# Two of four expert weight buffers held in a finished input tensor, early rows loaded from ScalarE's queue, and loads of sums ahead of stores

## The chip, the cores and the metric

The kernel runs on one core of a Trainium2 chip. A core has five engines that work from queues of their own and wait for one another through semaphores: TensorE (PE) multiplies matrices, VectorE (DVE), ScalarE (ACT) and GpSimd (POOL) work on elements, and SyncE (SP) mainly starts transfers. Sixteen DMA engines move data between the device memory (HBM) and the on-chip memory (SBUF), which has 128 partitions. A DMA can be started from SP, ACT or POOL. The metric is the device time of one execution in microseconds (us), the median of several.

## The reference

A network of two layers, each with a mixing part and a part with experts, on x of 8 sequences x 512 tokens x 256 features in float32. Each part's output is added to its input and normalized:

```python
x = layernorm(x + L0_attn(x))   # three recurrent layers: conv, gates, scan, projection, rmsnorm
x = layernorm(x + L0_ffn(x))    # 8 experts, each takes its best T/8 tokens; a token keeps one expert
x = layernorm(x + L1_attn(x))   # 16-head attention, a relative bias added after the softmax, norm
x = layernorm(x + L1_ffn(x))    # 16 experts, each token uses its best 4
# L0_ffn, for the expert e of a token:  gate * (gelu(x @ W1[e]) @ W2[e])
# L1_ffn, over the four experts:  sum of c[e] * (gelu(x @ w1[e] + b1[e]) @ w2[e] + b2[e])
```

In both expert parts W1 is 256 x 512 and W2 is 512 x 256. T is 4096 tokens.

## The kernel before, in words

The tokens lie in SBUF as 32 chunks of 128 rows (`x_ext`: the features, then gates and indices). In an expert part, every token's row is written ("put", L721, an indirect DMA from POOL) into the list of its expert in HBM (`m0rows` in layer 0, `m1rows` in the last layer). A list is then worked off in tiles of 128 rows: 39 tiles in layer 0, 143 in the last layer. Empty rows (`none`) are written behind the end of each list by `end_list` (L758).

`Lists.run` (L830) works off the tiles of both layers. For tile t it needs the rows (`load`, L872 to L874, five buffers named `xg`) and the weights of the tile's expert (`weights`, L865 to L870, four buffers `ws` of 1.03 MB each: both matrices, the bias and a one-hot row). Which expert and which rows these are stands in a table in SBUF; `value` reads an entry into a register of SP, and the DMA uses it as its address. The first four tiles load weights unconditionally (L868), later ones only when the expert changes (L870). `turn` transposes the rows on PE and copies them (`xq`, L888); `first` makes 16 matmuls (L899) and four gelus on ACT (L905 with bias, L907 without); `second` makes eight matmuls (L921) and hands the result to `done`. In layer 0 `done` scatters it to `res` (L1131), in the last layer it adds it into `acc` in HBM (L1736), both by indirect DMA from POOL.

Both layers form part of their tiles early. In layer 0 the first eight tiles come from lists that hold only the first half of the tokens: once those 16 chunks' puts have landed, a copy on ACT (`m0full`, L740) releases the row loads. While those tiles run, the other puts go on, and later the ends are written. In the last layer the first 64 tiles come from the first five sequences, whose lists are formed while attention (L1441) still works on the other three. Attention's loop hands out small pieces of this routing work, "parts", between its own steps; the piece that belongs to sequence b is made by a function near L1318, and the last part of sequence 4 makes the early table.

The order of instructions on an engine is fixed when the kernel is built: by hand for attention's PE, ACT and DVE work and for POOL in `run`, and by a scheduler elsewhere. An engine starts its instructions in that order, so an instruction that waits holds up what follows. Completions of the DMAs from SP and ACT are counted on eight semaphores taken in turn: a DMA is issued only when the eighth before it has landed.

After the last tile, `token_choice_layer` (L1745 to L1761) loads the sums from `acc` in eight groups of four chunks (two loads a group, L1751, pool of six buffers for each of the two), adds them and the input with biases (L1756, L1757), normalizes (L59 to L68) and stores the group with four DMAs (L1761). `xT` is the layer's input transposed: two slabs (dc = 0, 1) of 4096 tokens along the free axis. It is read for the attention's projections and the routing of each sequence.

Of the kernel before, what the change touches and what calls it, by code (L numbers as in the profile page):

```python
# [10 lines left out]
F32 = mybir.dt.float32  # L11
# [6 lines left out]
P = 128  # L18
B, S, D = 8, 512, 256
T = B * S  # L20
NC = T // P
# [658 lines left out]
class Lists:  # L680
# [6 lines left out]
    def __init__(self, tc, ctx, name, E, NT, a):  # L687
        nc = tc.nc
        self.tc, self.nc, self.name, self.E, self.NT = tc, nc, name, E, NT
        rp = self.rp = ctx.enter_context(tc.tile_pool(name=f"{name}r", bufs=1))  # L690
        self.dram = ctx.enter_context(
            tc.tile_pool(name=f"{name}d", bufs=1, space=bass.MemoryType.DRAM)
        )
        self.rows = self.dram.tile([E * LT + P, RW], F32, name=f"{name}rows")
        self.written = []


        self.tabs, self.early, self.loads, self.grown = [], 0, [], None
        self.tri = rp.tile([P, P], F32, name=f"{name}tri")
        nc.sync.dma_start(self.tri, a["c_tri"])  # L700

        self.iot = rp.tile([P, E], F32, name=f"{name}iot")
        nc.sync.dma_start(self.iot, a["c_iota"][:E].partition_broadcast(P))
        self.pno = rp.tile([P, 1], F32, name=f"{name}pno")
        nc.sync.dma_start(self.pno, a["c_part"])
        self.pnw = rp.tile([P, 1], F32, name=f"{name}pnw")
        nc.vector.tensor_scalar_add(self.pnw, self.pno, -1.0)
        self.off = rp.tile([P, E], F32, name=f"{name}off")
        nc.vector.tensor_scalar_mul(self.off, self.iot, float(LT))
        self.ones = rp.tile([P, P], F32, name=f"{name}ones")  # L710
        nc.vector.memset(self.ones, 1.0)
        none = self.none = rp.tile([P, RW], F32, name=f"{name}none")
        nc.gpsimd.memset(none, 0.0)  # L713
        nc.gpsimd.iota(
            none[:, D + E1 : D + E1 + 2].bitcast(I32), pattern=[[0, 2]], base=T, channel_multiplier=1
        )
        nc.sync.dma_start(self.rows[E * LT :, :], none)
# [99 lines left out]
    def early_tiles(self):  # L817
# [9 lines left out]

        return 0.6, part

    def run(self, ctx, ident, w_pack, bias, done, taken=None, besides=None):  # L830

        tc, nc, E, NT, nm = self.tc, self.nc, self.E, self.NT, self.name
        wp = ctx.enter_context(tc.tile_pool(name=f"{nm}w", bufs=1))
        hp = self.hp
        psX = ctx.enter_context(tc.tile_pool(name=f"{nm}psX", bufs=2, space=PSUM))
        psH = ctx.enter_context(tc.tile_pool(name=f"{nm}psH", bufs=4, space=PSUM))
        psO = ctx.enter_context(
            tc.tile_pool(name=f"{nm}psO", bufs=1 if bias else 2, space=PSUM)  # L840
        )
        ws = [wp.tile([P, WPK], F32, name=f"{nm}ws{i}") for i in range(NW)]
        xgs, hTs = {}, {}

        def table(t):
            return [(t0, tab) for t0, tab in self.tabs if t0 <= t][-1]

        def entry(t):

            t0, _ = table(t)  # L850
            end = min([NT] + [self.early] * (t < self.early))
            i, k = divmod(t - t0, NW)
            size, more = divmod(end - t0, NW)
            return k * size + min(k, more) + i

        def value(t, n, hi):
            _, tab = table(t)
            i = entry(t)
            return nc.values_load_multi_w_load_instructions(
                tab[i : i + 1, n : n + 1],  # L860
                engines=[mybir.EngineType.SP], min_val=0, max_val=hi,
                skip_runtime_bounds_check_because="clamped where the table is made",
            )[1][0]

        def weights(t):  # L865
            w = w_pack.rearrange("e p f -> (e p) f")[bass.ds(value(t, 1, E * P - P), P), :]
            if t - table(t)[0] < NW:
                nc.sync.dma_start(ws[t % NW], w)  # L868
            else:
                nc.sync.dma_start(ws[t % NW], w, cond=value(t, 2, 1))  # L870

        def load(t):  # L872
            xgs[t] = hp.tile([P, RW], F32, tag="xg", bufs=NW + 1, name=f"{nm}xg_{t}")
            ins = nc.sync.dma_start(xgs[t], self.rows[bass.ds(value(t, 0, E * LT), P), :]).ins  # L874
            if t < self.early:

                for w in self.written:
                    tc.declare_no_dep(ins, w, reason="other rows, or before grown")
                tc.add_manual_dep(ins, self.grown.name, SYNC, reason="full tiles")
                self.loads.append(ins)  # L880

        def turn(t):
            xg = xgs[t]
            ps = psX.tile([P, DC, P], F32, tag="x", name=f"{nm}xp_{t}")
            for dc in range(DC):
                nc.tensor.transpose(ps[:, dc, :], xg[:, dc * P : (dc + 1) * P], ident)  # L886
            xq = hp.tile([P, DC, P], F32, tag="xq", name=f"{nm}xq_{t}")
            nc.vector.tensor_copy(xq, ps)  # L888
            xgs[t] = (xg, xq)

        def first(t):
            xg, xq = xgs[t]
            w = ws[t % NW]
            hT = hp.tile([P, FC, P], F32, tag="hT", name=f"{nm}hT_{t}")
            for fc in range(FC):
                ps = psH.tile([P, P], F32, tag="h", name=f"{nm}h_{t}_{fc}")
                for dc in range(DC):
                    o = dc * F + fc * P
                    nc.tensor.matmul(  # L899
                        ps, w[:, o : o + P], xq[:, dc, :],  # L900
                        start=(dc == 0), stop=(dc == DC - 1),
                    )
                o = DC * F + FC * D + fc
                if bias:
                    ins = nc.scalar.activation(hT[:, fc, :], ps, AF.Gelu, bias=w[:, o : o + 1])  # L905
                else:
                    ins = nc.scalar.activation(hT[:, fc, :], ps, AF.Gelu)  # L907
            hTs[t] = hT
            if taken:
                taken(t, xg, w)  # L910
                xgs[t] = None, None
            return ins.ins

        def second(t):
            xg, _ = xgs.pop(t)
            hT = hTs.pop(t)
            w = ws[t % NW]
            ps = psO.tile([P, D], F32, tag="o", name=f"{nm}o_{t}")
            for fc in range(FC):
                o = DC * F + fc * D  # L920
                nc.tensor.matmul(  # L921
                    ps, hT[:, fc, :], w[:, o : o + D], start=(fc == 0), stop=(fc == FC - 1)
                )
            done(t, xg, ps)


        for t in range(0 if bias else NW):
            weights(t)
        for t in range(NW):
            load(t)  # L930
            if bias:
                weights(t)
        turn(0)
        for t in range(NT + 1):
            if t < NT:
                ins = first(t)
            if t + 1 < NT:
                turn(t + 1)
            if t > 0:
                second(t - 1)  # L940
                if t + NW - 1 < NT:
                    load(t + NW - 1)
                    weights(t + NW - 1)
            if besides and t < NT:
                besides(t, ins)
# [211 lines left out]
class TokenChoice:  # L1157


    def __init__(self, tc, ctx, x_ext, xT, ident, eps5, acc, a):  # L1160
# [19 lines left out]
        self.eps3, self.eps5 = (ATT_EPS, e3), (LN_EPS, eps5)  # L1180
        self.rb = rp.tile([P, E1], F32, name="rb1")
        nc.sync.dma_start(self.rb, a["router_b"].partition_broadcast(P))
        self.b2_in = a["b2"]
        self.gam = rp.tile([P, D], F32, name="gam")
        nc.sync.dma_start(self.gam, a["gamma"].partition_broadcast(P))
        self.bet = rp.tile([P, D], F32, name="bet")
# [5 lines left out]
    def parts(self, b):  # L1192
# [125 lines left out]
        if b == SE - 1:  # L1318
            n, count = self.count("n6")
            L.done = L.rp.tile([P, E1], F32, name="done")  # L1320
            last = [count] + L.table(n, 0, 0) + [L.early_tiles()]
        return (
            [(0.0, beta)] + normalize_parts(nc, gp, ao, ao, G1, self.eps3, f"ao_{b}", b < SE)
            + [(0.0, gamma), None]
# [383 lines left out]
def token_choice_layer(R, w_pack, eps5, out):  # L1708

    tc, nc, L = R.tc, R.nc, R.L  # L1710
    with ExitStack() as ctx:
# [30 lines left out]
            L.run(tiles, R.ident, w_pack, True, done, taken, R.besides)  # L1742

        assert not R.rest
        fp = ctx.enter_context(tc.tile_pool(name="m1f", bufs=6))  # L1745
        psF = ctx.enter_context(tc.tile_pool(name="m1psF", bufs=3, space=PSUM))
        for g in range(NC // 4):
            ys = []
            for i in range(2):
                yt = fp.tile([P, 4, D], F32, tag=f"f{i}", name=f"f{i}_{g}")  # L1750
                nc.sync.dma_start(yt, R.sums[i][:, g * 4 : (g + 1) * 4, :])  # L1751
                ys.append(yt)
            ps = psF.tile([P, 4, D], F32, tag="f", name=f"xb_{g}")
            R.plus_biases(g, ps)
            y = ys[0]
            nc.vector.tensor_add(y, y, ys[1])  # L1756
            nc.vector.tensor_add(y, y, ps)  # L1757
            layernorm(nc, L.sm, y, y, 4, eps5, f"m1_{g}")
            rows = out[g * S : (g + 1) * S, :].rearrange("(i q e) d -> e i q d", q=G1, e=4)
# [116 lines left out]
```

## Time and profile before

| what | us |
|---|---|
| median of 3 runs | 2020.09 (2019.97 to 2020.74) |
| the profiled execution's own time | 2018.68 |
| its span | 2016.9 |
| PE busy | 1742.5 |
| DVE busy | 1135.0 |
| ACT busy | 1002.7 |
| POOL busy | 514.4 |
| mean granted TensorE clock | 0.926 |

The span runs from the first to the last recorded instruction; the profiled execution's time is a little longer than its span. A row of the timeline gives start and length in us, engine, line, operation, output and inputs, the number of instructions in it (x9) and, in brackets, how long the engine was idle before it and what released it. SPq is SP's own queue that starts DMAs: such a row tells when transfers were issued, not when they landed. PEld is the loading of weights into TensorE. The page's slices divide the span in 40 parts of 50.4 us, with a digit for the busy tenths of each.

### The profile page before, as it was taken

The page shows a single profiled execution, that of the slowest core. Times are in us where ns is not written, and L with a number is a line of the kernel's source. Part 1 is how long each engine was busy: PE and PEld are TensorE (multiplying, and loading weights), DVE is VectorE, ACT ScalarE, POOL GpSimd, SP SyncE. Part 2 cuts the span into 40 slices and gives each one's busy share as a digit, 9 for nine tenths or more (in the row PEclk, how much of TensorE's full clock was granted, in tenths as well). Part 3 has the DMA queues.
Part 4 walks back from the last instruction along what each step waited for, and adds up shares of the span by engine and source line. Part 5 has one row for each costly group of instructions (what it writes and reads, how often), then busy time and mean ns, then how long its engine had stood idle before and what let it go on. Part 6 is the DMA issues. An engine that isn't in the chain of part 4 may idle for free. (4 is left out here: it accounts for less than half of the span.)

```text
span 2016.9 us, 31168 instructions
## 1 busy us (share of the span) xinstructions
PE 1742.5 (86%) x10396; PEld 1136.3 (56%) x10396; DVE 1135.0 (56%) x2841; ACT 1002.7 (50%) x2167; POOL 514.4 (26%) x438
## 2 busy tenths in 40 slices
PE   7999995532799698999989999987999999999993
PEld 3555553331799493222222222223899989999983
DVE  6999998853122622676868776884434222222225
ACT  4899976500223411466666766655434333433333
POOL 1000000005222311001131422332666634444430
PEclk8999997655899797999999999998999999999997
DMA  9000000004644300000010111113776676656566
GB/s 358 34 0 1 1 0 1 32 7 172 234 136 139 109 1 21 14 16 15 25 53 16 57 47 31 54 45 115 197 172 135 144 190 142 137 116 144 109 157 181
DMA packets 107103, 179.66 MB, mean 89 GB/s; under 512 B 17005, under 2 KB 86847, under 8 KB 100160
## 3 DMA queue, kind: packets, MB, share of 16 engines
q1 hardware_dynamic: 73760, 129.45, 20.7%
q0 software_dynamic: 30176, 45.59, 11.5%
q10 hardware_dynamic: 3008, 2.63, 0.4%
q8 instruction: 84, 1.38, 0.3%
q14 instruction: 75, 0.61, 0.1%
HBM read 244.79 MB, written 62.98 MB: 153 GB/s over the span
## 5 line engine op out<-in xcount | busy, mean ns | idle before, releaser
L1677 DVE TENSOR_REDUCE nmx<-s 128x1 f32<-128x512 f32 x512 | 329.7, 685 | 162.2 <-PE t L1599 104.5
L1684 ACT ACTIVATE pe<-t 128x512 f32<-128x512 f32 x512 | 277.8, 594 | 210.1 <-PE t L1599 199.0
L905 ACT ACTIVATE m1hT<-m1h,m1ws 128x128 f32<-128x128 f32 x572 | 208.5, 367 | 308.9 <-PE m1h L899 270.9
L1587 PE MATMUL s<-kT,qT 32*128 32x512 f32 x1024 | 304.3, 669 | 54.5 <-ACT pe L1684 26.0
L1599 PE MATMUL t<-qA,kT 32*128 32x512 f32 x1024 | 293.2, 649 | 2.5 <-ACT pe L1684 2.0
L899 PEld LDWEIGHTS m1h<-m1xq,m1ws 128*128 128x128 f32 x2288 | 278.6, 193 | 12.6 <-issue 5.4
L1736 POOL DMA_INDIRECT acc<-y,at x143 | 221.0, 1546 | 250.8 <-DVE at L1729 189.9
L899 PE MATMUL m1h<-m1xq,m1ws 128*128 128x128 f32 x2288 | 281.7, 276 | 3.7 <-issue 2.2
L921 PE MATMUL m1o<-m1ws,m1hT 128*128 128x256 f32 x1144 | 273.4, 380 | 3.4 <-DVE at L1729 1.6
L921 PEld LDWEIGHTS m1o<-m1ws,m1hT 128*128 128x128 f32 x1144 | 205.6, 190 | 26.8 <-issue 3.6
L1587 PEld LDWEIGHTS s<-kT,qT 32*128 32x128 f32 x1024 | 81.9, 190 | 221.8 <-ACT pe L1684 173.6
L888 DVE COPY m1xq<-m1xp 128x256 f32<-128x256 f32 x143 | 60.5, 423 | 193.3 <-PE m1xp L886 114.4
L1735 DVE TENSOR_SCALAR y<-m1o,gt 128x256 f32<-128x256 f32 x143 | 69.1, 483 | 163.7 <-PE m1o L921 156.2
L721 POOL DMA_INDIRECT m1rows<-x_ext,slot x128 | 126.9, 992 | 119.7 <-ACT pe L1684 78.4
L1623 PE MATMUL po<-pe,V 128*17 128x512 f32 x1024 | 136.4, 605 | 1.2 <-ACT pe L1684 1.2
L1653 POOL TENSOR_TENSOR AO<-AO,on 128x256 f32<-128x256 f32 x32 | 23.5, 735 | 352.9 <-DVE on L1648 352.8
L907 ACT ACTIVATE m0hT<-m0h 128x128 f32<-128x128 f32 x156 | 42.9, 277 | 123.6 <-PE m0h L899 97.7
L713 POOL MEMSET m0none<- 128x276 f32 x1 | 0.3, 327 | 394.8 <-ACT table L673 394.8
L299 PE MATMUL gate<-xc,wi 128*128 128x512 f32 x192 | 92.2, 611 | 2.5 <-ACT junk L382 2.5
L299 PE MATMUL gate<-xc,wr 128*128 128x512 f32 x192 | 87.2, 608 | 7.2 <-issue 7.2
L899 PE MATMUL m0h<-m0xq,m0ws 128*128 128x128 f32 x624 | 79.9, 282 | 14.4 <-issue 11.8
L899 PEld LDWEIGHTS m0h<-m0xq,m0ws 128*128 128x128 f32 x624 | 78.2, 198 | 18.5 <-issue 16.3
(342 smaller groups left out, 2662.2 us busy)
## 6 DMA issues: line engine op xcount, KB each, us to landing
m1ws<-in_w_pack SPq DMA_DIRECT2D x143, 1034.0 KB
m0ws<-in_w_pack SPq DMA_DIRECT2D x39, 1034.0 KB
m1xg<-m1rows SPq DMA_DIRECT2D x143, 138.0 KB
acc<-zero SPq DMA_DIRECT2D x2, 4096.0 KB
f<-acc SPq DMA_DIRECT2D x16, 512.0 KB
m0xg<-m0rows SPq DMA_DIRECT2D x39, 138.0 KB
xT<-in_xT SPq DMA_DIRECT2D x4, 1024.0 KB
x_ext<-in_x SPq DMA_DIRECT2D x4, 1024.0 KB
```

The lines of the kernel that those rows point to most:

```text
L299: nc.tensor.matmul(ps, w[("wr", "wi")[g]][:, l, dc, oc * P : (oc + 1) * P], xcs[u][:, dc, b, :], start=(dc == 0), stop=(dc == DC - 1),)
L721: ins = self.nc.gpsimd.indirect_dma_start(out=self.rows[:, :], out_offset=bass.IndirectOffsetOnAxis(ap=place, axis=0), in_=row, in_offset= ...
L899: nc.tensor.matmul(ps, w[:, o : o + P], xq[:, dc, :], start=(dc == 0), stop=(dc == DC - 1),)
L905: ins = nc.scalar.activation(hT[:, fc, :], ps, AF.Gelu, bias=w[:, o : o + 1])
L921: nc.tensor.matmul(ps, hT[:, fc, :], w[:, o : o + D], start=(fc == 0), stop=(fc == FC - 1))
L1587: mm = nc.tensor.matmul(ps, qTs[u % NR][r, qc * P : (qc + 1) * P], kTs[u % NR][r, :], start=True, stop=True,)
L1599: mm = nc.tensor.matmul(ps, kTs[v % NR][r, kc * P : (kc + 1) * P], qAs[v][r, :], start=True, stop=True,)
L1623: mm = nc.tensor.matmul(po[h4 * HP : h4 * HP + VW, :], V[:, b * NQ + kc, 4 * g + h4, :], pes.pop((u, kc, h4)), start=(kc == 0), stop=(kc = ...
L1677: ins = nc.vector.tensor_reduce(at, ps, AX.X, ALU.max, negate=True)
L1684: ins = nc.scalar.activation(pe, ps, AF.Exp)
L1735: nc.vector.tensor_scalar_mul(y, ps, gt)
L1736: nc.gpsimd.indirect_dma_start(out=R.acc[t % 2][:, :], out_offset=bass.IndirectOffsetOnAxis(ap=at, axis=0), in_=y, in_offset=None, compute ...
```

## The change

1. Two of the last layer's four weight buffers are no longer allocated: they are the first 2068 columns (tokens 0 to 2067) of the two slabs of `xT`. The new method `hold` issues their first loads from SP as the last part of sequence 4's routing, in attention. `run` then allocates only the other two, and `weights` leaves out tiles 0 and 1. For that, the functions that read the table become methods (`of`, `value`, `weights_of`).
2. In layer 0 (`bias` is False), the row loads of the eight early tiles are issued from ACT instead of SP; each reads its address into a register of ACT first.
3. At the end, the pool of the sums has eight buffers for each of the two, and all sixteen loads are issued in a loop of their own, ahead of the groups' additions and stores.

By the built order of instructions, five of the eight row loads stand on ACT between the copy that releases them and the load of the gelu table; the sixth stands ahead of tile 3's gelus and waits for the scatter of result 0, since there are five row buffers; the seventh and eighth stand ahead of tile 4's gelus. On SP the ends of the lists come right behind the first four weight loads. In the last layer SP has both held loads in attention and then row loads 0, 1, 2, weights 2, rows 3, weights 3; the loads of the second biases, which stood between the first row load and the first weights, come around tile 20. On ACT the load of the gelu table and the gelus of the first two tiles come ahead of a normalization of four chunks (L124), which stood ahead of them.

```diff
@@ -696,6 +696,7 @@
         self.tabs, self.early, self.loads, self.grown = [], 0, [], None
+        self.held = []
         self.tri = rp.tile([P, P], F32, name=f"{name}tri")
         nc.sync.dma_start(self.tri, a["c_tri"])
@@ -827,11 +828,39 @@
         return 0.6, part
+    def of(self, t):
+        return [(t0, tab) for t0, tab in self.tabs if t0 <= t][-1]
+    def value(self, t, n, hi, engine=mybir.EngineType.SP):
+        t0, tab = self.of(t)
+        end = min([self.NT] + [self.early] * (t < self.early))
+        i, k = divmod(t - t0, NW)
+        size, more = divmod(end - t0, NW)
+        i += k * size + min(k, more)
+        return self.nc.values_load_multi_w_load_instructions(
+            tab[i : i + 1, n : n + 1],
+            engines=[engine], min_val=0, max_val=hi,
+            skip_runtime_bounds_check_because="clamped where the table is made",
+        )[1][0]
+    def weights_of(self, t, w_pack):
+        at = self.value(t, 1, self.E * P - P)
+        return w_pack.rearrange("e p f -> (e p) f")[bass.ds(at, P), :]
+    def hold(self, w_pack, at):
+        for t, dst in enumerate(at):
+            self.nc.sync.dma_start(dst, self.weights_of(t, w_pack))
+        self.held = at
     def run(self, ctx, ident, w_pack, bias, done, taken=None, besides=None):
         tc, nc, E, NT, nm = self.tc, self.nc, self.E, self.NT, self.name
+        table, value, weights_of = self.of, self.value, self.weights_of
         wp = ctx.enter_context(tc.tile_pool(name=f"{nm}w", bufs=1))
         hp = self.hp
         psX = ctx.enter_context(tc.tile_pool(name=f"{nm}psX", bufs=2, space=PSUM))
@@ -839,31 +868,16 @@
         psO = ctx.enter_context(
             tc.tile_pool(name=f"{nm}psO", bufs=1 if bias else 2, space=PSUM)
         )
-        ws = [wp.tile([P, WPK], F32, name=f"{nm}ws{i}") for i in range(NW)]
+        ws = [None] * len(self.held) + [
+            wp.tile([P, WPK], F32, name=f"{nm}ws{i}") for i in range(len(self.held), NW)
+        ]
+        ws[: len(self.held)] = self.held
         xgs, hTs = {}, {}
-        def table(t):
-            return [(t0, tab) for t0, tab in self.tabs if t0 <= t][-1]
-
-        def entry(t):
-
-            t0, _ = table(t)
-            end = min([NT] + [self.early] * (t < self.early))
-            i, k = divmod(t - t0, NW)
-            size, more = divmod(end - t0, NW)
-            return k * size + min(k, more) + i
-
-        def value(t, n, hi):
-            _, tab = table(t)
-            i = entry(t)
-            return nc.values_load_multi_w_load_instructions(
-                tab[i : i + 1, n : n + 1],
-                engines=[mybir.EngineType.SP], min_val=0, max_val=hi,
-                skip_runtime_bounds_check_because="clamped where the table is made",
-            )[1][0]
-
         def weights(t):
-            w = w_pack.rearrange("e p f -> (e p) f")[bass.ds(value(t, 1, E * P - P), P), :]
+            if t < len(self.held):
+                return
+            w = weights_of(t, w_pack)
             if t - table(t)[0] < NW:
                 nc.sync.dma_start(ws[t % NW], w)
             else:
@@ -871,7 +885,10 @@
         def load(t):
             xgs[t] = hp.tile([P, RW], F32, tag="xg", bufs=NW + 1, name=f"{nm}xg_{t}")
-            ins = nc.sync.dma_start(xgs[t], self.rows[bass.ds(value(t, 0, E * LT), P), :]).ins
+            q = nc.sync if bias or t >= self.early else nc.scalar
+            at = value(t, 0, E * LT, q.engine)
+            ins = q.dma_start(xgs[t], self.rows[bass.ds(at, P), :]).ins
             if t < self.early:
                 for w in self.written:
@@ -1180,7 +1197,7 @@
         self.eps3, self.eps5 = (ATT_EPS, e3), (LN_EPS, eps5)
         self.rb = rp.tile([P, E1], F32, name="rb1")
         nc.sync.dma_start(self.rb, a["router_b"].partition_broadcast(P))
-        self.b2_in = a["b2"]
+        self.b2_in, self.w_pack = a["b2"], a["w_pack"]
         self.gam = rp.tile([P, D], F32, name="gam")
         nc.sync.dma_start(self.gam, a["gamma"].partition_broadcast(P))
         self.bet = rp.tile([P, D], F32, name="bet")
@@ -1318,7 +1335,12 @@
         if b == SE - 1:
             n, count = self.count("n6")
             L.done = L.rp.tile([P, E1], F32, name="done")
-            last = [count] + L.table(n, 0, 0) + [L.early_tiles()]
+            at = [self.xT[:, dc, :WPK] for dc in range(DC)]
+            last = [count] + L.table(n, 0, 0) + [
+                L.early_tiles(), (0.0, lambda: L.hold(self.w_pack, at))
+            ]
         return (
             [(0.0, beta)] + normalize_parts(nc, gp, ao, ao, G1, self.eps3, f"ao_{b}", b < SE)
             + [(0.0, gamma), None]
@@ -1742,18 +1764,19 @@
             L.run(tiles, R.ident, w_pack, True, done, taken, R.besides)
         assert not R.rest
-        fp = ctx.enter_context(tc.tile_pool(name="m1f", bufs=6))
+        fp = ctx.enter_context(tc.tile_pool(name="m1f", bufs=NC // 4))
         psF = ctx.enter_context(tc.tile_pool(name="m1psF", bufs=3, space=PSUM))
+        ys = {}
         for g in range(NC // 4):
-            ys = []
             for i in range(2):
-                yt = fp.tile([P, 4, D], F32, tag=f"f{i}", name=f"f{i}_{g}")
-                nc.sync.dma_start(yt, R.sums[i][:, g * 4 : (g + 1) * 4, :])
-                ys.append(yt)
+                ys[g, i] = fp.tile([P, 4, D], F32, tag=f"f{i}", name=f"f{i}_{g}")
+                nc.sync.dma_start(ys[g, i], R.sums[i][:, g * 4 : (g + 1) * 4, :])
+        for g in range(NC // 4):
             ps = psF.tile([P, 4, D], F32, tag="f", name=f"xb_{g}")
             R.plus_biases(g, ps)
-            y = ys[0]
-            nc.vector.tensor_add(y, y, ys[1])
+            y = ys[g, 0]
+            nc.vector.tensor_add(y, y, ys[g, 1])
             nc.vector.tensor_add(y, y, ps)
             layernorm(nc, L.sm, y, y, 4, eps5, f"m1_{g}")
             rows = out[g * S : (g + 1) * S, :].rearrange("(i q e) d -> e i q d", q=G1, e=4)
```

## The prediction

> **What bounds the kernel now.** I read the page first. TensorE is busy for 86% of the span, so time can be won only where it stands idle for another reason. In the slices it does so in three places that the change touches: in the tenth and eleventh (454 to 554 us, digits 2 and 7: layer 0's experts start), in the 28th (1361 to 1411 us, digit 7: from attention into the last layer's experts) and in the last (3).
>
> ```profile
> PE 1742.5 (86%) x10396; PEld 1136.3 (56%) x10396; DVE 1135.0 (56%) x2841; ACT 1002.7 (50%) x2167; POOL 514.4 (26%) x438
> PE   7999995532799698999989999987999999999993
> ```
>
> Then the timeline of each place. First the end of the program, where nothing overlaps, so that a microsecond won is a microsecond of the span:
>
> ```profile
> 1959.07 4.35 SPq L1751 DMA_DIRECT2D f<-acc  x9
> 1973.33 16.10 SPq L1761 DMA_DIRECT2D out<-f  x20
> 1977.61 1.19 DVE L1756 TENSOR_TENSOR f<-f,f 128x1024 f32<-128x1024 f32 x1
> 1984.83 2.07 ACT L68 ACTIVATE f<-f,mr_m,rs_m 128x256 f32<-128x256 f32 x4 [0.44 <-DVE mr_m L66]
> 1989.48 2.77 SPq L1751 DMA_DIRECT2D f<-acc  x5
> 1994.97 1.22 DVE L1756 TENSOR_TENSOR f<-f,f 128x1024 f32<-128x1024 f32 x1 [10.18 <-DMA f<-acc]
> 2004.03 9.81 SPq L1761 DMA_DIRECT2D out<-f  x12
> 2008.99 2.07 ACT L68 ACTIVATE f<-f,mr_m,rs_m 128x256 f32<-128x256 f32 x4 [0.44 <-DVE mr_m L66]
> ```
>
> Nine loads of sums go out at once, then SP sits in 20 stores, each of which waits for its group's normalization, and only at 1989.48 come the five loads left. VectorE idles 10.18 us for them. Second, the start of the last layer's experts, in the timeline and in windows of 5 us (columns: length, busy time of PE, its weight load, DVE, ACT, POOL, granted clock, DMA share, GB/s):
>
> ```profile
> 1387.59 0.36 SPq L874 DMA_DIRECT2D m1xg<-m1rows  x1
> 1390.80 1.27 SPq L1415 DMA_DIRECT2D b<-in_b  x3
> 1394.28 0.36 SPq L868 DMA_DIRECT2D m1ws<-in_w_pack  x1
> 1400.06 3.73 PE L899 MATMUL m1h<-m1xq,m1ws 128*128 128x128 f32 x16
> 1401.38 1.28 ACT L905 ACT_TABLE_LOAD   x1 [0.30 <-ACT x_ext L124]
> 1390.00:1395.00 5.00, 1.51 (x6) 1.14 (x6) 4.10 (x19) 0.26 (x1) 2.38 (x3) 0.50 0.04 10
> 1395.00:1400.00 5.00, 0.39 (x2) 0.42 (x3) 4.89 (x44) 1.00 (x3) 0.00 (x0) 0.50 0.91 319
> 1400.00:1405.00 5.00, 5.00 (x24) 4.91 (x24) 3.13 (x24) 4.41 (x10) 0.00 (x0) 0.50 1.00 400
> ```
>
> The first weights are asked for at 1394.28, behind the bias loads and a release by POOL, and land at about 1400, when the first matmul starts. Third, layer 0's start:
>
> ```profile
> 490.69 12.70 SPq L874 DMA_DIRECT2D m0xg<-m0rows  x4
> 507.62 9.48 SPq L758 DMA_DIRECT2D m0rows<-m0none  x8
> 501.34 0.28 ACT L907 ACTIVATE m0hT<-m0h 128x128 f32<-128x128 f32 x1 [5.04 <-issue]
> 511.17 0.28 ACT L907 ACTIVATE m0hT<-m0h 128x128 f32<-128x128 f32 x1 [9.55 <-remote]
> 507.68 0.97 POOL L721 DMA_INDIRECT m0rows<-x_ext,slot  x1 [0.30 <-issue]
> 516.47 1.95 PE L899 MATMUL m0h<-m0xq,m0ws 128*128 128x128 f32 x16
> ```
>
> Four row loads take SP 12.7 us, while a later one takes about 0.86 with its address. ACT's gelus creep too, though matmuls are done. Both recover when POOL's last put (507.68) has landed; the profile names no releaser.
>
> **What the Trainium skill says.** "DMA: Bandwidth & Descriptors", section "Issuing engines are not separate DMA queues": starting DMAs from several engines saves only the sequencer's time, since all share the 16 DMA engines. So row loads on ACT can win no more than SP's issue time; here that is 12.7 us in a disturbed stretch. "PSUM — Partial Sum Buffer", section "Engine vs sequencer instructions": ScalarE's queue is strict FIFO; a load that waits holds up the gelus behind it. "TensorE: Matmul & The Clock Gate", Part 1: half clock until about 3.4 us of sustained work; the trace agrees (0.50 until 1405, sixteen L899 matmuls in 3.73 us against 1.95 warm).
>
> **The change, part by part.** All sums are against the profiled execution: 2018.68 us, span 2016.9, 1.41 us under the median of 2020.09.
>
> *Tail.* Sixteen loads go ahead of every store and have buffers of their own. Loads: 16 x 0.524 MB = 8.4 MB; the window 1965 to 1970 moves 415 GB/s, so they take 20.2 us and the last lands, some 2 us of start added, at about 1981. At most eight are under way, as SP's completion semaphores go round by eight; so the last is issued when the eighth lands, about 1971, before the first store is ready (1973.33). No store is made late. A group costs VectorE 4.0 us (the adds of the fourth and fifth start at 1973.62 and 1977.61). The sixth then starts at 1981.6, the eighth at 1989.6, later than its data. The fifth took 1984.83 + 2.07 - 1977.61 = 9.3 us from first add to last activation, so ACT ends at 1998.9, and the end follows 5.84 us later (2016.9 - 2011.06) at 2004.7: **-12.2 us**. If the rate falls to 300 GB/s once stores share it, the last load lands at 1987, still in time. Ends: -10 (only part of the idle 10.18) and -13.
>
> *Two held buffers.* Their 2.1 MB go out from SP at about 1344, behind batch 4's parts, where DMA is busy for 0.15 to 0.23 (windows of 1340 to 1360); the row loads of the early list wait for the fence at 1366 anyway, so nothing on SP is late. At 1387 what remains for tile 0 is its row load (issued 1387.59), transpose and the copy to xq, which ended at 1395.1; its first matmul can start at 1395.4 instead of 1400.06: -4.7. The clock is still 0.50 there, so 3.73 us stay. In the new order the gelu table (1.28 us, a step that stays) and tile 0's gelus come ahead of ACT's x_ext normalization, which moves POOL's two 2.35 us steps (1407.82 and 1410.25) and the router's VectorE block about as much later: tile 3, which waited for that block (copy at 1414.19), gets through first, tile 5 meets it. Without a cover a held-up tile costs one step of 3.7, so of 4.7 I keep **-4**; ends -1.5 and -7. The other two buffers' loads come earlier too, and the bias loads move to about tile 20, where SP has slack (a tile lasts 3.73, SP's part about 1.2).
>
> *Layer 0.* SP loses eight row loads (22 sequencer steps), ACT gains 24. Five loads (15 steps) stand ahead of the gelu table; the sixth, ahead of tile 3's gelus, reuses tile 0's rows and waits until POOL's scatter of result 0 has landed; so do the seventh and eighth for results 1 and 2, ahead of tile 4's. The empty list ends come 12.7 us earlier on SP. In this stretch each sequencer step of SP and of ACT takes some 0.7 us (the single rows of the trace, 0.03 to 0.3 elsewhere). If that stays, the five loads cost 15 x 0.7 = 10.5 us, putting tile 0's gelus at about 503 to 506 instead of 496. But the first gelus of tile 1 were spread to 512.6 already, and ACT's backlog can be worked off in 0.45 us steps; tile 2's matmuls come at about 515 instead of 516.5, later tiles follow that. I take **-2**; ends +4 (the sixth load holds tile 3 for one scatter, 2.75 us, and a step) and -11 (next paragraph).
>
> Sum: -12.2 - 4 - 2 = -18.2: profiled about 2000.5, median about 2002.
>
> **The rivals.** *Stall gone.* If the creep comes from SP's and ACT's steps meeting and the new order avoids it, gelus go at 496 to 498, result 0 is scattered at 509 (after the last put, 507.68 + 1.28) and lands 2.75 later, tile 3's gelus run at 512 and tile 4's matmuls at about 514 instead of 524.4: -10.5. Sum -26.7: about 1993.5. For it: ACT and SP recover together. Against: they recover with the puts, which stay.
> *Layer 0 pays.* The waits on ACT add 3 to 4 us there and the held buffers' gain shrinks to 3: -12.2 - 3 + 3.5 = about -12: 2008.
> *Tail limited by DMA.* If 8.4 MB of loads and five groups' stores (2.6 MB) moved at only 330 GB/s, the eighth group's data would land at 1959.1 + 33.4 = 1992.5 instead of the 1989.6 that VectorE needs: tail -9.3, sum -15.3: about 2005. Against: the loads of before ran at 415.
> *Slower.* One mechanism: ACT's creep with five loads ahead of its gelus. Half a tile is not enough: to undo 16.2 us of the other two parts, tile 2's matmuls must come after 516.5 + 16.2 = 532.7, so the table after about 530. That is 39 us for 15 steps, 2.6 us each, nearly four times 0.7, and lasting 20 us past the last put. At 3.5 us a step the time would be 2018.68 - 16.2 + 30 = 2032. Against: nothing in the profile creeps once the puts have landed.
>
> **How the numbers follow.** Likeliest sum (with the tail limit within it) 0.50, stall gone 0.25, layer 0 pays 0.12, tail limited 0.07, slower side 0.04, no difference 0.02. Predicted: 2002. The range runs from 1991 (stall gone, with a larger second part) to 2009 (layer 0 pays, tail -10 and so on): some 0.85. Differences under 0.2%, about 4 us, are what a measurement of this kernel can't tell from none: faster 0.94, within 0.2% 0.02, slower 0.04. The likeliest's own range is 1999 to 2006.
>
> **What would show it.** Right: no idle of VectorE over 2 us after the first add of the tail, all 16 loads ahead of the first store and an end near 45.5 us after the first load (57.8 before); first L899 matmul about 8 us after the first row load's issue (12.5 before); tile 2 of layer 0 no later than 26 us after the ACT fence (516.47 - 490.47). Wrong: gaps of several us between the tail's adds, a first matmul still waiting for the weights' DMA, or the table load of layer 0 after 510 and gelus waiting for ACT's own row loads. What would break the sum most is layer 0, whose stall I can time but not explain.

## The result, and the profile after

The changed kernel takes 2002.66 us (1999.21 to 2006.98, five runs) against 2020.09 before (five runs, 2018.07 to 2020.74): ratio 0.9918, interval 0.9903 to 0.9933, or 17 us less. The profiled execution fell from 2018.68 to 2001.20 us, its span from 2016.9 to 1999.4. Forecast were 2002, with 18.2 us less. The total was right; the stages below show that not every term of it was. In the experiments, one execution of 3481 us (of the kernel with the tail and the held buffers) is counted as slow, and its ratio stands on the other three.

First the timeline of the end of the changed kernel:

```profile
1948.52 16.23 SPq L1774 DMA_DIRECT2D f<-acc  x16
1958.14 1.23 DVE L1779 TENSOR_TENSOR f<-f,f 128x1024 f32<-128x1024 f32 x1 [10.28 <-DMA f<-acc]
1968.33 28.05 SPq L1784 DMA_DIRECT2D out<-f  x32
1984.51 1.21 DVE L1779 TENSOR_TENSOR f<-f,f 128x1024 f32<-128x1024 f32 x1
1991.77 2.08 ACT L68 ACTIVATE f<-f,mr_m,rs_m 128x256 f32<-128x256 f32 x4 [0.44 <-DVE mr_m L66]
```

All sixteen loads are issued ahead of the first store, and VectorE has no bracket of idle time on a later first add: the eighth group's starts at 1984.51, without waiting. From the first add to the end it is 41.3 us (1999.4 - 1958.14) instead of 54.1 (2016.9 - 1962.78).

Second, the start of the last layer's experts, and the held loads in attention:

```profile
1342.52 1.44 SPq L855 DMA_DIRECT2D xT<-in_w_pack  x2
1387.70 2.00 SPq L891 DMA_DIRECT2D m1xg<-m1rows  x3
1395.33 3.77 PE L916 MATMUL m1h<-m1xq,xT 128*128 128x128 f32 x16 [1.68 <-DVE m1xq L905]
1396.63 1.28 ACT L922 ACT_TABLE_LOAD   x1 [4.25 <-PE m1h L916]
```

The first matmul starts at 1395.33, 4.7 us earlier, and what releases it is the copy of the rows, no longer the weights. Since tile 1's weights are held as well, the lead grows: tile 2's copy of rows comes 12.9 us after attention's end instead of 21.5. Tile 5 gives most of it back. Its copy, at 1417.71, stands on VectorE behind the statistics of a normalization (the block that the prediction names), and these wait for POOL:

```profile
1416.02 1.08 DVE L89 BATCH_NORM_STATS2 st_ax<-x_ext 128x6 f32<-128x256 f32 x3 [4.11 <-POOL x_ext L1231]
```

It comes 7.1 us after tile 4's (3.4 before), 31.3 us after attention's end instead of 34.6.

Third, layer 0. The first line is of the kernel before, the others of the changed one:

```profile
490.68 1.28 ACT L907 ACT_TABLE_LOAD   x1
481.75 32.43 SPq L759 DMA_DIRECT2D m0rows<-m0none  x8
493.96 18.92 ACTq L891 DMA_DIRECT2D m0xg<-m0rows  x5
512.92 1.28 ACT L924 ACT_TABLE_LOAD   x1 [21.68 <-DMA m0rows<-m0none]
```

Here the creep, the sequencer steps of some 0.7 us that the prediction describes, fell on ACT's loads as well as on SP. ACT's five loads take 18.92 us, and the gelu table comes only at 512.92, where before it came at 490.68.

The stages of the two executions, taken from the starts of VectorE's copies of rows (one a tile, `xq`) and the end of attention's last exponential, in us:

| stage | before | after | difference |
|---|---|---|---|
| start to ACT's release copy | 490.5 | 491.0 | +0.6 |
| release to layer 0's tile 38 | 164.3 | 167.9 | +3.6 |
| tile 38 to the last exponential of attention | 731.6 | 727.5 | -4.1 |
| from there to tile 25 of the last layer | 114.3 | 113.1 | -1.2 |
| tile 25 to tile 142 | 446.2 | 442.6 | -3.6 |
| tile 142 to the end | 70.05 | 57.26 | -12.8 |

The sum is -17.5. Two rows were in no part of the forecast: the 4.1 us ahead of attention's end, of which 4.0 lie ahead of its first exponential (157.0 us after tile 38 instead of 161.0), where the change has no edit; and the 3.6 us that came long after the first tiles.

**Where the 3.6 us of the tiles come from.** The spacings of the copies differ at tiles 56 to 61 alone. TensorE's timeline there, of the kernel before and then of the changed one:

```profile
1635.91 1.10 PE L921 MATMUL m1o<-m1ws,m1hT 128*128 128x256 f32 x4 [0.67 <-DVE junk L1725]
1636.85 1.95 PE L899 MATMUL m1h<-m1xq,m1ws 128*128 128x128 f32 x16
1638.86 1.03 PE L921 MATMUL m1o<-m1ws,m1hT 128*128 128x256 f32 x4
```

```profile
1633.93 1.95 PE L916 MATMUL m1h<-m1xq,m1ws 128*128 128x128 f32 x16
1635.93 1.89 PE L938 MATMUL m1o<-m1ws,m1hT 128*128 128x256 f32 x8
```

Before, the scheduler had split the eight second matmuls of a tile around the next tile's first ones. The part put ahead waits for VectorE's copy out of the only accumulator, and tiles 59 to 61 take 5.07, 5.07 and 5.50 us instead of 3.73. In the kernel built with the change the order is regular there.

**Where the 4.1 us ahead of attention come from.** VectorE and POOL, before and then after:

```profile
681.41 4.66 POOL L1210 TENSOR_TENSOR x_ext<-x_ext,bet 128x1024 f32<-128x1024 f32 x2 [16.82 <-PE tp L143]
681.88 1.92 DVE L709 TENSOR_SCALAR m1off<-m1iot 128x16 f32<-128x16 f32 x1
683.77 2.38 DVE L1472 TENSOR_SCALAR pick<-m1pno 128x128 f32<-128x128 f32 x1
```

```profile
686.07 6.99 POOL L1227 TENSOR_TENSOR x_ext<-x_ext,bet 128x1024 f32<-128x1024 f32 x3 [17.27 <-DMA bet<-in_beta]
685.94 0.22 DVE L1494 TENSOR_SCALAR pick<-m1pno 128x128 f32<-128x128 f32 x1
```

An operation of VectorE that takes 0.2 us takes 2.38 beside POOL's addition. The Trainium skill ("SBUF — State Buffer", section "SBUF: two separate sides") says that VectorE and GpSimd have a port pair in common, which one of them holds for a whole instruction while the other blocks, where VectorE's operation uses two ports or has two inputs in SBUF. The durations agree: the two operations end at 683.80 and 686.15, POOL's two additions at 683.76 and 686.07. Before, five small operations of VectorE met one of POOL's additions in this stretch (1.7 to 2.4 us each). After, POOL's first addition waited for the load of `bet`, and four met. In all fourteen traces (these two and the twelve of the experiments below) five meetings go with 160.7 to 161.6 us from tile 38 to the first exponential, and four with 156.5 to 157.7, once 159.4. The operations that met take 10.2 us together in the kernel before and 7.4 in the changed one: 2.8 of the 4.0 us. What the rest is was not found.

### The profile page after: what moved, and what is told of

The parts are those of the page before. It is cut to its first block, busy times and chain, and to the rows that moved or that the text cites. A ratio compares the mean times of both kernels' runs of the same rounds, so it can differ in the third digit from the quotient of the medians.

```text
span 1999.4 us, 31165 instructions
## 1 busy us (share of the span) xinstructions
PE 1737.9 (87%) x10396; PEld 1135.0 (57%) x10396; DVE 1130.2 (57%) x2841; ACT 1004.5 (50%) x2167; POOL 515.3 (26%) x438
## 5 line engine op out<-in xcount | busy, mean ns | idle before, releaser
L922 ACT ACTIVATE m1hT<-m1h,m1ws 128x128 f32<-128x128 f32 x284 | 104.0, 369 | 155.2 <-PE m1h L916 133.6
L922 ACT ACTIVATE m1hT<-m1h,xT 128x128 f32<-128x128 f32 x288 | 105.9, 369 | 148.5 <-PE m1h L916 133.6
L1757 DVE TENSOR_SCALAR y<-m1o,gt 128x256 f32<-128x256 f32 x143 | 69.1, 483 | 167.9 <-PE m1o L938 161.1
L916 PE MATMUL m1h<-m1xq,xT 128*128 128x128 f32 x1152 | 143.5, 278 | 4.7 <-issue 3.0
L916 PEld LDWEIGHTS m1h<-m1xq,xT 128*128 128x128 f32 x1152 | 141.3, 194 | 9.4 <-issue 3.8
L916 PEld LDWEIGHTS m1h<-m1xq,m1ws 128*128 128x128 f32 x1136 | 137.4, 192 | 7.5 <-issue 4.1
L916 PE MATMUL m1h<-m1xq,m1ws 128*128 128x128 f32 x1136 | 138.7, 275 | 2.9 <-DVE m1xq L905 2.2
L938 PE MATMUL m1o<-xT,m1hT 128*128 128x256 f32 x576 | 138.2, 382 | 0.7 <-issue 0.5
L938 PE MATMUL m1o<-m1ws,m1hT 128*128 128x256 f32 x568 | 134.9, 379 | 0.0
L938 PEld LDWEIGHTS m1o<-xT,m1hT 128*128 128x128 f32 x576 | 104.2, 192 | 12.2 <-ACT m1hT L922 0.7
L938 PEld LDWEIGHTS m1o<-m1ws,m1hT 128*128 128x128 f32 x568 | 102.2, 190 | 10.8
```

The lines of the kernel that those rows point to most:

```text
L916: nc.tensor.matmul(ps, w[:, o : o + P], xq[:, dc, :], start=(dc == 0), stop=(dc == DC - 1),)
L938: nc.tensor.matmul(ps, hT[:, fc, :], w[:, o : o + D], start=(fc == 0), stop=(fc == FC - 1))
L1757: nc.vector.tensor_scalar_mul(y, ps, gt)
```

## The experiments

They ran on other chips, where the kernel before took 2001.6 to 2004.7 us in the median. In none of their twelve profiles do SP and ACT creep in layer 0: from ACT's release copy to tile 2's copy it is 10.0 to 14.0 us, against 24.2 and 27.6 in the first two. So ratios are compared, within each chip. The theory going in: tail -12.8, held buffers -4.8 and ACT's rows about nothing in the end; the rival: ACT's rows cost 4 us, which a chance meeting hid.

### The three parts alone

The tail's edit alone:

```diff
-        fp = ctx.enter_context(tc.tile_pool(name="m1f", bufs=6))
+        fp = ctx.enter_context(tc.tile_pool(name="m1f", bufs=NC // 4))
...
+        for g in range(NC // 4):
+            for i in range(2):
+                ys[g, i] = fp.tile([P, 4, D], F32, tag=f"f{i}", name=f"f{i}_{g}")
+                nc.sync.dma_start(ys[g, i], R.sums[i][:, g * 4 : (g + 1) * 4, :])
```

> The kernel before with the tail's edit alone. Theory (the three parts add up as the two traces show them): the time falls by 12.8 us (from the last tile's copy to the end 57.3 us instead of 70.1), to about 2007. Rival (the tail's gain rests on the row of other shifts, for example on a DMA queue that is emptier by then): less than 10.

Measured: 0.9954 (0.9934 to 0.9973), 9.2 us less. The interval, 5.4 to 13.2 us, holds the theory's 12.8 and the rival's less than 10; the traces say more. The stage after tile 142 takes 57.24 us here, and in the two profiles of the same chip with the old tail 67.75 and 68.18: 10.5 and 10.9 us. Over all fourteen profiles it takes 67.8 to 70.9 us in six with the old order and 56.9 to 58.8 in eight with the new one, 12.0 us in the mean.

The held buffers alone, that is, the changed kernel with the old tail and this line:

```diff
-            q = nc.sync if bias or t >= self.early else nc.scalar
+            q = nc.sync
```

> The kernel before with the two held buffers alone. Theory: 4.8 us less, to about 2015, the tiles of layer 0 untouched. Rival (the gain at the first tile is given back at the router's block): under 2 us.

Measured: 0.9956 (0.9923 to 0.999), 8.8 us less, with a wide interval (2.0 to 15.4 us) that holds the theory and ends at the rival. Over all profiles with the scheduler's own order, the stretch from attention's end to tile 142 takes 560.5 to 564.4 us in four kernels without held buffers and 552.1 to 557.6 in seven with them: 6.8 in the mean. Of these, 3.7 us are tiles 56 to 62 (29.8 against 26.1, the same within 0.1 in each group).

ACT's row loads alone, that is, the kernel before with:

```diff
-            ins = nc.sync.dma_start(xgs[t], self.rows[bass.ds(value(t, 0, E * LT), P), :]).ins
+            q = nc.sync if bias or t >= self.early else nc.scalar
+            at = value(t, 0, E * LT, q.engine)
+            ins = q.dma_start(xgs[t], self.rows[bass.ds(at, P), :]).ins
```

> The kernel before with layer 0's early row loads on ACT alone. Theory: tiles 2 to 38 of layer 0 run 3.5 to 4 us later, as in the changed kernel, and the time moves by -1 to +1, because the stretch between layer 0's end and the attention loop takes the delay up. Rival (what took it up was a chance meeting of VectorE and POOL in that execution): 2 to 4 us more, about 2023.

Measured: 1.0023 (1.0007 to 1.0039), 4.6 us more: the rival. The stretch ahead of attention took nothing up. It is longer, 729.3 us from tile 38 to attention's end against 725.5 in the kernel with held buffers alone, with five meetings of VectorE and POOL against four. ACT's timeline in this kernel, without creep:

```profile
491.83 4.79 ACTq L891 DMA_DIRECT2D m0xg<-m0rows  x5
496.71 1.28 ACT L924 ACT_TABLE_LOAD   x1 [5.89 <-DMA m0xg<-m0rows]
512.91 0.35 ACTq L891 DMA_DIRECT2D m0xg<-m0rows  x1
513.36 0.79 ACT L924 ACTIVATE m0hT<-m0h 128x128 f32<-128x128 f32 x4 [7.05 <-DMA res<-z,m0xg]
```

and in the kernel with the tail alone, where SP loads:

```profile
494.49 0.28 ACT L907 ACTIVATE m0hT<-m0h 128x128 f32<-128x128 f32 x1 [4.57 <-PE m0h L899]
504.63 0.67 ACT L907 ACTIVATE m0hT<-m0h 128x128 f32<-128x128 f32 x2 [2.17 <-PE m0h L899]
509.39 0.66 ACT L907 ACTIVATE m0hT<-m0h 128x128 f32<-128x128 f32 x2 [3.20 <-PE m0h L899]
```

With rows on ACT the first gelu comes at 498.0, 7.4 us after the release copy (490.6), against 6.1 (494.49 - 488.4). Tile 3's gelus wait behind the sixth load, which result 0 holds up, and start 22.7 us after the release (513.36 - 490.6) instead of 16.2 (504.63 - 488.4); tile 4's, at 509.39 with rows on SP, are later still. From tile 5 on less of it is left, since with rows on SP the sixth rows wait for result 0 as well, but on SP, with the gelus of tiles 0 to 4 done by then: tile 8's copy comes 43.9 us after the release, against 37.5 to 41.5 with rows on SP. At tile 38 it is 156.3 us here and 156.9 in the changed kernel without creep, against 151.2 to 156.5 in six kernels with rows on SP, 153.8 in the mean. So some 2.8 us of the cost are seen in layer 0 in the mean, at the edge of the scatter of the six; whether the fifth meeting, which adds to it behind tile 38, is a consequence of the later rows was not tested.

Tail and held buffers, rows on SP (the changed kernel with the line above):

> The changed kernel with all row loads on SP again. Theory: layer 0 is as before, and the time is that of the changed kernel within 1 us (about 2002), since the delay in layer 0 did not reach the end. Rival (the delay is real and was hidden by chance in the one execution profiled): 3 to 4 us less than the changed kernel, about 1998.5.

Measured: 0.9894 (0.9863 to 0.9926), 21 us less. The intervals of this and of the changed kernel overlap, so this run alone doesn't decide; the one before, whose interval (1.4 to 7.8 us) leaves out the theory's +1, speaks for the rival.

### What rows on ACT cost, and why

The changed kernel beside three others on one chip:

> The changed kernel as it is, beside the next three. Theory (the rows on ACT cost some 4 us net of everything behind them): about 0.9915 of the kernel before. Rival (the earlier executions met by chance): within 0.1% of the kernel with the tail and the held buffers alone, 0.9895.

Measured: 0.9923 (0.9906 to 0.9939). The theory holds: the recorded gain repeats on a chip without creep.

Nine row buffers in layer 0, rows on ACT and then rows on SP:

```diff
-            xgs[t] = hp.tile([P, RW], F32, tag="xg", bufs=NW + 1, name=f"{nm}xg_{t}")
+            xgs[t] = hp.tile([P, RW], F32, tag="xg", bufs=NW + 1 if bias else NE0 + 1, name=f"{nm}xg_{t}")
```

> The changed kernel with nine row buffers in layer 0 instead of five, so that no early row load waits for a scatter of results. Theory (the cost is ACT's wait: the sixth load, ahead of tile 3's gelus, waits until result 0 has landed, 7 us): the cost is gone, tile 8 starts no later than 38 us after ACT's release copy, against 44 with rows on ACT and five buffers, and the time is within 1 us of the next kernel's. Rival (the cost is the issue time of the loads ahead of the gelu table, now eight loads, some 8 us): 4 us or more slower than the next kernel.

> Tail and held buffers, rows on SP, nine row buffers in layer 0. Theory (also on SP the sixth load waits for result 0, which POOL scatters only after its last put): tile 5's copy comes 2.5 us earlier than with five buffers, and the time is 2 to 3 us below that of tail and held buffers alone. Rival (tile 8 waits for the fence behind POOL's scatters anyway): no difference.

Measured: 0.9892 (0.9874 to 0.9909) with ACT, 0.9878 (0.9861 to 0.9894) with SP; the medians are 1982.57 and 1978.70, with four executions each, whose ranges overlap a little (1979.85 to 1983.18 and 1975.38 to 1980.41). From the release copy to tile 8 it takes (us):

| | rows on ACT | rows on SP |
|---|---|---|
| five buffers | 43.9 and 44.9 | 37.5 to 41.5 |
| nine buffers | 39.5 | 35.3 and 35.7 |

At tile 8 both reasons hold, each for a part. Nine buffers take away ACT's wait and, on the same chip, 5.5 us with it (44.9 against 39.5). What is left between ACT and SP, 4.2 us at tile 8 and already 3.9 at tile 2 (14.0 against 10.1), goes with the eight loads that now stand on ACT ahead of the first gelu (7.62 us from the first issue to the last, and the first gelu 10.2 us after the release instead of 5.8). So the theory of the wait alone, which asked for a difference within 1 us and for tile 8 at 38 us, was too narrow; the rival's 4 us are just missed by the medians' 3.9. With rows on SP, nine buffers bring tile 5's copy from 25.0 to 22.8 us after the release and tile 38's from 151.2 to 147.3. The theory's 2 to 3 us of time are not shown: the intervals with five and with nine buffers overlap (0.9863 to 0.9926, 0.9861 to 0.9894), and the two ran on different chips.

Sixteen later puts spread over tiles 0 to 3:

```diff
-            for c in range(NC // 2, NC):
-                L.put(slot[:, c : c + 1], x_ext[:, c, :])
...
+            if t < NE0 - NW:
+                for c in range(NC // 2 + 4 * t, NC // 2 + 4 * t + 4):
+                    L.put(slot[:, c : c + 1], x_ext[:, c, :])
```

> Tail and held buffers, rows on SP, and the second half's sixteen puts of layer 0 issued four a tile behind tiles 0 to 3 instead of all at once ahead of the first result. Theory (POOL's puts hold result 0 back and with it the sixth row load): result 0 is scattered some 8 us earlier, tiles 5 to 8 follow, 3 to 6 us less than tail and held buffers alone. Rival (the sequencers of SP and ACT creep while POOL puts, wherever the puts stand): in a trace where they creep, steps of 0.7 us are seen behind each group of puts, and nothing is won.

Measured: 0.9907 (0.989 to 0.9923), no gain. Result 0 is scattered 13.6 us after the release instead of 18.8 (kernel with tail and held buffers), and tile 5's copy comes 2.2 us earlier (22.8 against 25.0). But the fence on POOL, for which tile 8's rows wait, comes behind the last puts at 34.4 us instead of 28.0, and tile 8's copy at 41.5 us, the upper end of what rows on SP show with five buffers (37.5 to 41.5). There was no creep in this profile, so the question of its cause was not reached.

### The scheduler's order, and buffers against order in the tail

TensorE's order in the last layer's tiles as written:

```diff
-            L.run(tiles, R.ident, w_pack, True, done, taken, R.besides)
+            with tc.manual_schedule(engines={mybir.EngineType.PE}):
+                L.run(tiles, R.ident, w_pack, True, done, taken, R.besides)
```

It was put on the kernel before, on the best kernel so far, and on the held buffers alone.

> The kernel before with TensorE's order in the last layer's tiles fixed as written (a tile's eight second matmuls whole, then the next tile's sixteen). Theory (half of what the changed kernel won in the last layer's tiles came from the scheduler's order at tiles 56 to 61, not from the held buffers): the spacings of 5.0 to 5.7 us at tiles 45 to 47 and 59 to 61 become 3.73, about 4.5 and 3.6 us less, together 8 us, 0.4%. Rival (those spacings come from DMA or the expert changes there): unchanged.

> Tail, held buffers, rows on SP with nine buffers, and TensorE's order as written: the version to which the runs so far point. Theory: 4.5 us less than without the fixed order (tiles 44 to 46), about 0.9855 of the kernel before. Rival (the router's matmuls among the first 30 tiles are placed worse when the order is fixed): no gain or a loss.

> The two held buffers alone, with TensorE's order as written. Against the kernel before with that order alone it shows what the held buffers are worth by themselves. Theory: 1 to 2 us (the first tiles start 9 us earlier after the first copy, the router's block takes most of it back by tile 25). Rival (the recorded sum): 4 us.

Measured: 0.9988 (0.9979 to 0.9996), 0.9892 (0.9876 to 0.9909) and 0.9993 (0.9979 to 1.0006). The theory's local part holds: on the kernel before, tiles 44 to 48 take 14.9 us instead of 19.6, and 55 to 62 take 26.8 instead of 29.8, without held buffers. So the slow spacings are the order's, not the transfers'. As a version it is no gain. On the kernel before, the whole is 2.4 us less instead of 8, since the written order is slower elsewhere: 27.0 us instead of 25.3 from tile 48 to 55, and 300.2 instead of 298.5 from tile 62 to 142. With the held buffers, the copy of tile 5 comes 35.6 and 36.7 us after attention's end, no earlier than without (35.4), where the scheduler's order had 31.3 to 31.8. In the written order two groups of the router's matmuls stand ahead of tile 1's and wait 2.43 us for VectorE there; tile 2's copy comes 20.1 us after attention's end with held buffers, against 13.1 in the scheduler's order. What the held buffers are worth "by themselves" therefore depends on the order: some 1 to 4 us at the start with the scheduler's (33.0 to 35.8 against 31.3 to 31.8 at tile 5), nothing at tile 5 with the written one; at tile 142 the written order has 560.2 us without and 559.8 and 556.8 with them, too scattered to tell. The times of the first and the third run show no difference (0.9988 and 0.9993); in their profiles VectorE met POOL five times ahead of attention in the third and four times in the first.

Eight buffers for the sums without the new order:

```diff
-        fp = ctx.enter_context(tc.tile_pool(name="m1f", bufs=6))
+        fp = ctx.enter_context(tc.tile_pool(name="m1f", bufs=NC // 4))
```

> The kernel before with eight buffers for the sums instead of six and the statements' order left. Theory (SP's order, five loads behind twenty stores, is what costs, not the buffers): the tail as before, about 68 to 70 us from the last tile's copy to the end, no difference. Rival (buffers): 10 us less.

Measured: 1.0006 (0.9997 to 1.0014). SP's order stays:

```profile
1934.88 9.91 SPq L1751 DMA_DIRECT2D f<-acc  x11
1954.67 16.12 SPq L1761 DMA_DIRECT2D out<-f  x20
1970.83 2.81 SPq L1751 DMA_DIRECT2D f<-acc  x5
```

Five loads are still behind twenty stores. Buffers alone gain nothing; the tail's gain needs the order. The order with six buffers was not run.

The lowest ratio measured is that of tail, held buffers, rows on SP and nine row buffers: 0.9878, some 24 us less than before. Its interval overlaps those of its nearest neighbours (five buffers, nine with rows on ACT, TensorE's order as written), so its lead over them is not shown. It leaves out one of the change's three parts.

## Why the prediction was right, and where it was not

**Tail: right, mechanism and size.** -12.2 forecast, -12.8 in the trace. Its steps hold: the loads land in time, a group costs VectorE 4.0 us (first adds at 1980.5 and 1984.5 in the pace of the groups before), the last group takes 9.3 us from first add to last activation (1984.51 to 1993.85), and the end follows 5.6 us later. The 0.6 us more are small terms: seven groups took 26.4 us from first add to first add instead of the 26.8 reckoned, and the last stores 5.55 instead of 5.84. One reading was wrong without harm: the line of nine loads begins at the third. Eleven loads go out ahead of the stores, the first at 1953.17, which with the five later ones makes sixteen. So the forecast 45.5 us are from the third load to the end, and there they are 45.1 (1999.4 - 1954.31).

**Held buffers: the start right, its remainder too large, another gain not seen.** The first matmul is 4.7 us earlier, as forecast, at the clock of 0.50 as forecast: it lasts 3.77 us. (The half clock held until 5.9 us after the first matmul before, longer than the 3.4 that the prediction goes by, and until 3.6 us after it in the changed kernel.) Also as forecast, tile 5 met the router's block. But the lead ahead of that block was 8.6 us at tile 2, not 4.7, and more than one step was lost to it and behind it. The step "of 4.7 I keep **-4**" failed: in this pair of profiles 1.2 us are left at tile 25, less than the weakest end forecast, -1.5; over all kernels with the scheduler's order it is about 3 (115.9 us from attention's end to tile 25 in the mean of four without held buffers, 112.7 in the mean of seven with them, each group scattered by 4 to 6). The other 3.6 us come from TensorE's built order at tiles 56 to 61. The orders of both kernels could be compared ahead of time, and the prediction compares the first tiles only. Since this gain was in no part of the sum, the total of the part, -4.8 against -4, was met by luck.

**Layer 0: the step with the wrong sign.** "I take -2" was +3.6 in the trace, near the upper end of +4. The working had both costs, 10.5 us of issue ahead of the gelus and the wait of the sixth load, and then waved the first away with "ACT's backlog can be worked off". Its own sign of being wrong, "the table load of layer 0 after 510", came true at 512.92. The creep on ACT took 18.9 us for five loads rather than 10.5, tile 2 came 3.4 us later after the release instead of 1.5 earlier, and tile 8 6.8 us later. In layer 0 that is the rival "layer 0 pays", which had 0.12. On a chip without creep the same part by itself costs 4.6 us of the whole time (1.4 to 7.8).

**A cover that nobody planned.** With +3.6 in layer 0 and nothing else unforeseen ahead of attention, the sum would have been about -13. It was -17.5, since the stretch ahead of attention was 4.1 us shorter, where VectorE met POOL's additions once less. That the total came out within 1 us was luck: layer 0 missed its term by 5.6 us, and a gain that no part of the sum contains made up for most of that. The theory with which I went into the experiments, that this stretch takes such a delay up, fell: with rows on ACT three of four profiles have five meetings there, with rows on SP two of ten. Whether the later arrival makes the five likelier is open; no run fixed the meeting.

**The other rivals.** "Stall gone" did not come: the creep stayed and moved to ACT too. "Tail limited by DMA" did not come either. The slower side did not come: the table was loaded at 513, not after 530.

**Open.** Why SP and ACT step every 0.7 us for 20 us in the two profiles of the first chip. No run elsewhere had it, so none could test it. That it ends some 5 us after POOL's last put starts (507.68 and 512.5 before, 507.61 and 512.9 after) was seen, and its cause is not shown. By tile 2 the kernel before is 13 to 14 us behind six kernels with the same row loads on other chips (24.2 us after the release against 10.0 to 11.3), by tile 38 still 8 to 13 (164.3 against 151.2 to 156.5). So the creep goes with about half or more of the 15 to 19 us between this chip's time before and the others'; the kernel before itself was not profiled there.

## What to carry to other kernels

A queue that starts transfers is also an order: loads without a dependence go ahead of stores that wait for computed groups, and extra buffers do nothing until the order lets them be used. Before row loads are moved to an engine that computes, count the loads ahead of its first operation and ask which of them waits; here the relieved queue was not what held the time. And where a scheduler builds the order, compare the orders of the whole stage: an edit at the first tile changed the spacing at tile 59.

## What the hardware showed that was not expected

- VectorE's small operations took 1.4 to 2.4 us instead of 0.15 to 0.22 when they met POOL's addition of 128x1024 (2.34 us). One meeting more or less went with about 4 us at the start of attention (its first exponential 157 us after layer 0's last tile, 159 once, against 161), with no edit there.
- The same kernel took 2020.1 us on one chip and 2001.6 to 2004.7 on three others. On the first chip there was a stretch of 20 us in which instructions of 0.03 us on SP and ACT took 0.7; by tile 38 of layer 0 that chip was 8 to 13 us behind.
- A row load with its address from a table costs ACT about 1.1 us from one issue to the next (five issued from 491.83 to 496.27), and SP about 0.9 (four in 2.98 us).
